# Layer 0 aggregates normalized tokens first and applies its weights behind each panel

## The chip, the core and the metric

The kernel runs on one core of one Trainium2 chip. The metric is the time of one execution on the device, in microseconds. Three runs of the kernel before took 1234.97, 1236.31 and 1237.64 us; the median is 1236.31 us.

Engines are named as the profile names them: PE is TensorE (PEld its weight load), DVE is VectorE, ACT is ScalarE, POOL is GpSimd and SP is SyncE, which issues most DMAs.

## The reference, cut to what matters

3327 tokens with 256 features pass two layers; each layer is a graph step and a mixture of experts. The change is in the graph step of layer 0, the first work of the program:

```python
# --- layer 0 ---
#   support = layernorm(x) @ W
#   out = relu(adj @ support + b)
x = x + _L0_gnn_ref(_layernorm(x, axis=-1), adj, L0_gnn_W, L0_gnn_b)
x = x + _L0_ffn_ref((_layernorm(x, axis=-1))[None], ...)[0]    # 8 experts, 2 per token, hidden 1024, ReLU
# --- layer 1: the same two kinds of step, adjacency filtered by tanh(adj * adj) and top 700 ---
```

`adj @ (layernorm(x) @ W)` equals `(adj @ layernorm(x)) @ W`, so the product with the weights can stand on either side of the aggregation. Layer 1 keeps at most 700 neighbours of a node, so the kernel counts the positive entries of each row of `adj` while it has them in memory.

## The kernel before, in words

All matrices are fp32. Tokens are padded to 3328: 26 tiles of 128 tokens, held in `x` as `[128, 26, 256]`. The transposed adjacency is cut into 13 panels of 256 nodes (`PW`); a panel holds all 3328 source tokens in two pieces of 13 tiles each (`CJ`), 1.66 MB a piece. Pieces live in a ring of six places (`RING`), so three panels are in memory at a time.

**The program is scheduled by a list scheduler at build time.** It orders the instructions of each engine by the order of the code and by its own estimate of when they are ready; every engine's queue, SP's and POOL's included, is then worked strictly in order. `tc.issue_after(ins)` and the helper `behind(list)` force what is traced inside them to come later than a given instruction on its engine's queue. DMAs of SP are issued in order, and one whose target place is not free holds all those behind it.

**Start (lines 132 to 150, 239 to 254, 1044 to 1062).** SP loads `x` in groups of tiles and the weights `proj_sb`; then the six pieces of panels 0 to 2. PE runs 32 small bf16 products on a constant (`WARM`). POOL loads biases and four small arrays of layer 1 (`f1_r_sb`, `g1_bp_sb`, `f1_b1_sb`, `g1_wg_sb`). For each group of token tiles DVE computes `statistics` (`bn_stats` and `bn_aggr` for each tile, then a chain of 12 small dependent operations on the whole group, lines 270 to 279: the inverse square root of the variance by three Newton steps). PE turns every raw tile (line 305), ACT copies the turned pair out (line 306), PE multiplies by the weights, from which the column mean is taken off once (`ps_mean`, line 1053), and ACT writes the node features `s` scaled by the inverse deviation (line 318). So `s` is `layernorm(x) @ W`, ready for all 26 tiles before the first panel.

**Panels (`aggregate`, lines 345 to 368).** For each panel and each half of 128 nodes PE sums 26 products into one PSUM tile, an adjacency block stationary and `s[:, j, :]` moving (line 359). `add_relu` on DVE adds the bias and the ReLU to `x`. Then `after0(pan)` routes the panel's tokens: a layernorm, scores against eight gates by 16 `rt_product` operations on DVE (line 379), the two best, an `Exp` on ACT (line 444), and the queueing of a list. `list_waiting` works that list a panel later: two pairs of small products on PE (lines 465 and 466), some DVE work, and four scatters of token rows on POOL into the experts' lists `xlist0` in DRAM. ACT does 16 `Sign` operations per panel with a running sum (`count`, line 1069), which read the panel's pieces in the ring: a place is free for the next load only once PE and ACT are both done with it.

**Side work on the queues.** `after0(0)` turns the two gate matrices in DRAM with element-wise DMAs on SP (line 1085), loads the first with a broadcast on POOL (`load_gate`, line 247), and `fill` writes default rows into both token lists: 32 DMAs on SP (lines 1035 and 1037) from a tile that POOL prepares. At the end of the last panels the first experts' weights are loaded into free places of the ring (`layer0.load`).

**The seam to the experts (`step`, lines 934 to 946).** A step works one block of 256 rows of one expert: `first` (products into `ps_h`, bias and ReLU on ACT), then the next block's rows are turned (line 861) and copied by DVE (line 864), then `second` (products into `ps_y`, DVE, a scatter on POOL). Two steps run after the last panel, then `list_waiting` for its tokens, then the plan for the remaining blocks.

PSUM is shared by tags: `ph` (two tiles: `ps_h`, `ptb`), `py` (four: `ps_g`, `ps_s`, `ps_y`, `ps_warm`), `pt` (two).

Of the kernel before, what the change touches and what calls it, by code (L numbers as in the profile page):

```python
# [10 lines left out]
F32 = mybir.dt.float32  # L11
BF16 = mybir.dt.bfloat16
# [63 lines left out]


BEGUN, FIRST_TILES, MORE_TILES = 12, 14, 22
WARM = 32
TIERS = 3  # L80
# [10 lines left out]
def gnn_moe_two_layers(  # L91
# [38 lines left out]
    cum = state.tile([P, NT + 1, E], BF16, name="cum")  # L130

    proj_sb = const.tile([P, DC, D], F32, name="proj_sb")
    for t, n in [(0, 2)] + [(t, 4) for t in range(2, NT, 4)]:
        nc.sync.dma_start(out=x[:, t : t + n, :], in_=x_in[:, t : t + n, :])
        if t == 0:
            nc.sync.dma_start(out=proj_sb, in_=g0_w.rearrange("(c p) n -> p c n", p=P))


# [7 lines left out]
    make_identity(nc, ident)  # L146
    mean = ring[RING - 1][:, 0:P]
    nc.gpsimd.memset(mean, 1.0 / D)
    ones = const.tile([P, 1], F32, name="ones")
# [92 lines left out]

    f1_r_sb = by_feature("f1_r_sb", f1_rT)
    gates = []

    def load_gate(g):
# [4 lines left out]

    g1_bp_sb = plain("g1_bp_sb", g1_bp)
    f1_b1_sb = plain("f1_b1_sb", f1_b1)
    g1_wg_sb = by_feature("g1_wg_sb", g1_wg)

# [52 lines left out]

    def node_features(i, lhsT, w_sb, scale=None):

        ps = psy.tile([P, D], F32, name="ps_s", tag="py")
        for c in range(DC):
            nc.tensor.matmul(
                ps, lhsT=lhsT[:, c, :], rhs=w_sb[:, c, :], start=(c == 0), stop=(c == DC - 1)
            )
        if scale is None:
            return nc.scalar.copy(s[:, i, :], ps)
        return nc.scalar.activation(s[:, i, :], ps, AF.Copy, scale=scale)

# [10 lines left out]

    def piece(pan, k):
        return ring[(pan * NCHUNK + k) % RING].rearrange("p (c w) -> p c w", w=PW)

    last_piece, output_loads = [], []

    def load_panel(pan, prepare, earlier=()):

        for k in range(NCHUNK):
            a = piece(pan, k)
            with behind(earlier):  # L340
                d = nc.sync.dma_start(out=a, in_=adjT[pan, k])
            last_piece[:] = [d]
            prepare(pan, k, a)

    def aggregate(b_sb, prepare, after, loaded=0, count=None):

        for pan in range(NPAN):
            while loaded < min(pan + RING // NCHUNK, NPAN):
                load_panel(loaded, prepare)
                loaded += 1  # L350
            chunks = [piece(pan, k) for k in range(NCHUNK)]
            if count:
                count(pan, chunks)
            ps = [psy.tile([P, D], F32, name="ps_g", tag="py") for _ in range(PW // P)]
            for k in range(NCHUNK):
                for it in range(PW // P):
                    for c in range(CJ):
                        j = k * CJ + c
                        nc.tensor.matmul(  # L359
                            ps[it],  # L360
                            lhsT=chunks[k][:, c, ts(it, P)],
                            rhs=s[:, j, :],
                            start=(j == 0),
                            stop=(j == NT - 1),
                        )
            for it in range(PW // P):
                add_relu(x[:, pan * (PW // P) + it, :], ps[it], b_sb)
            after(pan)

    def rows_of(a, t0, n):  # L370
# [382 lines left out]
    def experts(xlist, ys, group, fixed, n_hidden, func, w1T, b1, w2T, b2, copy, kept=None):  # L753
# [179 lines left out]

        def step(late, end=always, place=None):

            t = len(started)
            started.append(t)
            while len(loaded) < min(t + RING // places, end):
                load(late)
            if t not in ready:  # L940
                ready[t] = turned(loaded[t][1], groups_of(t))
            _, _, w1, bb1, _, _ = loaded[t]
            hT = first(ready.pop(t), w1, bb1, groups_of(t))
            if t + 1 < min(len(loaded), end):
                ready[t + 1] = turned(loaded[t + 1][1], groups_of(t + 1), place)
            second(t, late, hT)
# [68 lines left out]
    def fill(*lists):  # L1015


        with tc.issue_after(last_feature.ins):
            wide = blk.tile([P, H // P, SB], F32, name="wide").rearrange("p h b -> p (h b)")
# [12 lines left out]
            for xlist in lists:  # L1032
                for e in range(E):
                    first = xlist[e * NP : e * NP + SB, :].rearrange("(g p) d -> p g d", p=P)
                    nc.sync.dma_start(out=first[:, :, 0:ID], in_=zeros)
                    with nc.allow_non_contiguous_dma("two elements of a partition"):
                        nc.sync.dma_start(
                            out=first[:, :, ID : ID + 1], in_=rows_f[:, e, :].unsqueeze(2)
                        )

    deviation = {}
    for t0, n0 in [(0, 2), (2, 2), (4, 4), (8, 4), (12, 6), (18, 8)]:
        _, rs = statistics(t0, n0)
        deviation.update((t0 + g, rs[:, g : g + 1]) for g in range(n0))
        for t in range(t0, t0 + n0, 2):
            xT = turned_tiles([x[:, t + g, :] for g in range(2)])
            if t == 0:  # L1050
                ps = psy.tile([P, D], F32, name="ps_mean", tag="py")
                for c in range(DC):
                    nc.tensor.matmul(
                        ps, lhsT=mean, rhs=proj_sb[:, c, :], start=(c == 0), stop=(c == DC - 1)
                    )
                nc.vector.tensor_tensor(
                    proj_sb, proj_sb, ps.unsqueeze(1).to_broadcast([P, DC, D]), ALU.subtract
                )
            for g in range(2):
                last_feature = node_features(  # L1060
                    t + g, xT[:, :, ts(g, P)], proj_sb, deviation[t + g]
                )

    def count(pan, chunks):
        with tc.issue_after(last_feature.ins):
            for k, a in enumerate(chunks):
                for i in range(PW // GROUP):
                    sign = work.tile([P, CJ, GROUP], BF16, name="sign", bufs=1)
                    nc.scalar.activation(  # L1069
                        sign, a[:, :, ts(i, GROUP)], AF.Sign, bias=below,  # L1070
                        accum_out=positive[:, pan, i, k : k + 1],
                    )
# [6 lines left out]
    def after0(pan):  # L1079
        if pan == 0:  # L1080
            with tc.issue_after(last_piece[0].ins):
                for name, w in (("gate0", f0_wgT), ("gate1", f1_rT)):
                    g = dram.tile([E, D], F32, name=name)
                    with nc.allow_non_contiguous_dma("a few thousand elements"):
                        nc.sync.dma_start(out=g.rearrange("e d -> d e"), in_=w)
                    gates.append(g)
            load_gate(gates[0])
            fill(xlist0, xlist1)
        if FREE_PAN <= pan < NPAN - 1:
            layer0.load(None)  # L1090
        t, n = PAIRS[pan]
        list_waiting()
        xn = layernorm(t, n)
# [6 lines left out]

    aggregate(gnn_b_sb, lambda pan, k, a: None, after0, count=count)

    layer0.step(None)
    layer0.step(None)
# [418 lines left out]
```

## Time and profile before

| what | value |
|---|---|
| median of three runs | 1236.31 us (1234.97 to 1237.64) |
| the profiled execution's own time | 1235.14 us |
| its span | 1233.4 us |
| PE, PEld busy | 1198.3, 1037.4 us |
| DVE, ACT, POOL busy | 698.1, 522.6, 271.7 us |
| first product of the first panel | 41.03 us |
| first product of the first expert block | 335.41 us |
| DMA, mean over the span | 196 GB/s |

Times are counted from the start of the span. In a row of the order of time come the start, the duration of the merged group, the engine, the line, the operation, its tiles (out<-in), shape and count; in brackets stands the idle time before it and what ended that. Matmuls are pipelined and their ends are modelled, so pace is read from the distance of starts. A row of windows gives each engine's busy time in a stretch, the clock granted to PE (1.00 is full), the share of the 16 DMA engines in use and what they moved. Some matmul records can be missing.

### The profile page before, as it was taken

How to read it: one execution, taken by the hardware profiler on the slowest of the kernel's cores; microseconds unless marked ns; L12 is line 12 of the kernel's file. 1: busy time of each engine (PE TensorE's matmuls, PEld its weight loads, DVE VectorE, ACT ScalarE, POOL GpSimd, SP SyncE). 2: the span in 40 equal slices, each digit the busy share in tenths (PEclk: the TensorE clock that was granted, in tenths of full speed). 3: DMA queues.
4: the chain of work that ended last, by engine and by line, in shares of the span. 5: the costliest groups of instructions: out<-in, count | busy, mean ns of one | idle time of the engine just before them, and what ended most of it. 6: DMA issues, size and time to landing. Idle time of an engine off the chain costs nothing. (4 is left out here: it accounts for less than half of the span.)

```text
span 1233.4 us, 18208 instructions
## 1 busy us (share of the span) xinstructions
PE 1198.3 (97%) x5853; PEld 1037.4 (84%) x5853; DVE 698.1 (57%) x2812; ACT 522.6 (42%) x963; POOL 271.7 (22%) x339
## 2 busy tenths in 40 slices
PE   8999999999999999999999999999999999999973
PEld 7888888888888888888888888888888888888862
DVE  6057877677664111211121167568999999786453
ACT  4869545541022222322222225896455453043331
POOL 2003131131231111111111110002323223255531
PEclk9999999999999999999999999999999999999996
DMA  9696455454167655766657657244445442477695
GB/s 349 187 241 246 176 201 176 147 191 142 63 233 231 208 195 175 240 201 204 233 179 229 224 223 268 79 167 172 164 177 195 161 158 90 128 245 248 209 288 195
DMA packets 122537, 241.59 MB, mean 196 GB/s; under 512 B 24352, under 2 KB 92992, under 8 KB 115392
## 3 DMA queue, kind: packets, MB, share of 16 engines
q1 hardware_dynamic: 107760, 205.33, 50.1%
q0 software_dynamic: 11136, 31.60, 7.0%
q10 hardware_dynamic: 3536, 3.41, 0.8%
q8 instruction: 48, 0.79, 0.3%
q14 instruction: 57, 0.47, 0.1%
HBM read 203.98 MB, written 36.33 MB: 195 GB/s over the span
## 5 line engine op out<-in xcount | busy, mean ns | idle before, releaser
L359 PE MATMUL ps_g<-s,ring 128*128 128x256 f32 x2704 | 588.2, 380 | 0.0
L359 PEld LDWEIGHTS ps_g<-s,ring 128*128 128x128 f32 x2704 | 512.0, 190 | 68.7
L873 PE MATMUL ps_h<-xT,ring 128*128 128x256 f32 (+1 forms) x1176 | 251.1, 366 | 3.3 <-ACT xT L864 2.1
L873 PEld LDWEIGHTS ps_h<-xT,ring 128*128 128x128 f32 x1176 | 205.6, 191 | 40.6 <-ACT wide L880 5.8
L880 ACT ACTIVATE wide<-ps_h,ring 128x256 f32<-128x256 f32 (+1 forms) x240 | 110.3, 460 | 283.9 <-PE ps_h L873 283.0
L379 DVE SCALAR_TENSOR_TENSOR rt_product<-xn,gate 128x256 f32<-128x256 f32 x400 | 198.0, 495 | 12.4
L912 PE MATMUL ps_y<-ring,wide 128*128 128x256 f32 x896 | 200.3, 379 | 0.0
L483 POOL DMA_INDIRECT xlist<-xn,rt_idx x104 | 106.4, 1023 | 398.6 <-DVE ln_ve L270 281.8
L912 PEld LDWEIGHTS ps_y<-ring,wide 128*128 128x128 f32 x896 | 167.1, 190 | 21.0
L1069 ACT ACTIVATE sign<-ring,below 128x416 bf16<-128x416 f32 x208 | 133.5, 642 | 66.4 <-DMA ring<-in_adjT 60.2
L483 POOL DMA_INDIRECT ys<-narrow,index x56 | 55.1, 985 | 330.9 <-DVE narrow L920 238.1
L1220 ACT ACTIVATE ring<-ring 128x3328 f32<-128x3328 f32 x22 | 65.4, 2979 | 87.2 <-DVE ring L1219 56.6
L864 DVE COPY xT<-ptb 128x512 f32<-128x512 f32 (+1 forms) x29 | 19.0, 654 | 147.0 <-PE ptb L861 147.0
L919 DVE TENSOR_TENSOR narrow<-ps_y,ring 128x256 f32<-128x256 f32 x56 | 23.8, 424 | 133.7 <-PE ps_y L912 130.7
L323 DVE TENSOR_TENSOR gnn_t<-ps_g,gnn_b_sb 128x256 f32<-128x256 f32 x52 | 21.9, 420 | 112.1 <-PE ps_g L359 99.0
L483 POOL DMA_INDIRECT ys<-wide,index x58 | 58.2, 1004 | 60.1 <-DVE wide L920 34.5
L1221 ACT ACTIVATE ring<-ring 128x3328 f32<-128x3328 f32 x22 | 65.4, 2977 | 0.6
L444 ACT ACTIVATE rt_d<-rt_d 128x2 f32<-128x2 f32 x26 | 5.3, 202 | 117.3 <-DVE rt_d L443 117.3
L912 PE MATMUL ps_y<-s,narrow 128*128 128x256 f32 (+1 forms) x200 | 49.3, 387 | 0.1
L267 DVE BATCH_NORM_STATS2 ln_st<-x 128x6 f32<-128x256 f32 x104 | 42.9, 419 | 4.0 <-DMA x<-in_x 2.9
L861 PE MATMUL ptb<-ident,ring 128*128 128x128 f32 x228 | 36.3, 279 | 5.3 <-ACT narrow L880 5.1
L1219 DVE TENSOR_SCALAR ring<-ring 128x3328 f32<-128x3328 f32 x22 | 41.3, 1883 | 0.0
(215 smaller groups left out, 964.2 us busy)
## 6 DMA issues: line engine op xcount, KB each, us to landing
ring<-in_adjT SPq DMA_DIRECT2D x52, 1664.0 KB, 7.6
ring<-in_f_w1T SPq DMA_DIRECT2D x30, 1024.0 KB, 6.2
ring<-in_f_w2T SPq DMA_DIRECT2D x30, 1024.0 KB, 8.1
ring<-xlist SPq DMA_DIRECT2D x52, 258.0 KB, 3.1
ring<-in_f_w SPq DMA_DIRECT2D x36, 256.0 KB, 3.6
ring<-ys SPq DMA_DIRECT2D x14, 512.0 KB, 4.2
ring<-in_f_b SPq DMA_DIRECT2D x34, 128.0 KB, 7.5
xlist<-wide SPq DMA_DIRECT2D x16, 257.0 KB, 6.3
```

The costliest lines, as they stand in the source:

```text
L267: nc.vector.bn_stats(out=st, in_=x[:, t0 + g, :])
L359: nc.tensor.matmul(ps[it], lhsT=chunks[k][:, c, ts(it, P)], rhs=s[:, j, :], start=(j == 0), stop=(j == NT - 1),)
L379: nc.vector.scalar_tensor_tensor(product, xn[:, g, 0, 0:D], 1.0, gate[:, e, :], ALU.mult, ALU.mult, accum_out=sc[:, g, e : e + 1],)
L483: d = nc.gpsimd.indirect_dma_start(out=a[:, :], out_offset=bass.IndirectOffsetOnAxis(ap=index, axis=0), in_=rows_, in_offset=None,)
L861: nc.tensor.transpose(pt[:, c, ts(g, P)], xb[:, g, ts(c, P)], ident)
L873: nc.tensor.matmul(ps, lhsT=w1[:, c, ts(hc, P)], rhs=xT[:, c, :], start=(c == 0), stop=(c == DC - 1),)
L880: nc.scalar.activation(hT[:, hc, :], ps, func, bias=bb1[:, hc : hc + 1])
L912: last_product[:] = [nc.tensor.matmul(ps, lhsT=hT[:, hc, ts(g, P)], rhs=w2[:, hc, :], start=(hc == 0), stop=(hc == hc_n - 1),)]
L1069: nc.scalar.activation(sign, a[:, :, ts(i, GROUP)], AF.Sign, bias=below, accum_out=positive[:, pan, i, k : k + 1],)
L1219: nc.vector.tensor_scalar(a, a, 0.0, None, ALU.max)
L1220: nc.scalar.activation(a, a, AF.Square)
L1221: nc.scalar.activation(a, a, AF.Tanh)
```

## The change

The order of weights and aggregation is swapped for layer 0.

- `s` becomes `layernorm(x)` itself, written by DVE; the transposes, the feature products, `ps_mean` and ACT's copies before the panels go. The first four groups of tiles are put strictly one behind the other on DVE's queue; the last two are not.
- `aggregate_first` sums transposed panels: `s[:, j, c]` (128 tokens, 128 features) is stationary and 256 columns of the adjacency move; each panel has two sums, one for each half of the features. Panels 0 and 1 run together, tile by tile, through their first pieces.
- When a panel's sums are complete ACT copies them out (`g`). In the next panel, after six token tiles (`BEHIND`), PE multiplies `g` by the weights, and `add_relu` and `after0` follow (`finish`). The last panel's `finish` goes between `first` and the next block's turn in the first expert step.
- SP loads `x` in five groups, with the matching parts of the first pieces of panels 0 and 1 behind the first four. The weights and the first gate's turn stand behind panel 1, the second gate's behind panel 2.
- The counts of a panel stand behind the copies of the panel before on ACT's queue. The small loads stand behind the first layernorms in the code. `fill` runs for one list at panel 1 and for the other at panel 4, behind the latest pieces. The list of panel 0 is worked together with that of panel 1. 54 products warm PE instead of 32.

```diff
+BEHIND = 5
-WARM = 32
+WARM = 54
...
-    for t, n in [(0, 2)] + [(t, 4) for t in range(2, NT, 4)]:
+    for t, n in [(0, 2), (2, 2), (4, 4), (8, CJ - 8), (CJ, NT - CJ)]:
         nc.sync.dma_start(out=x[:, t : t + n, :], in_=x_in[:, t : t + n, :])
-        if t == 0:
-            nc.sync.dma_start(out=proj_sb, in_=g0_w.rearrange("(c p) n -> p c n", p=P))
+        if t < CJ:
+            for pan in range(2):
+                nc.sync.dma_start(
+                    out=piece(pan, 0)[:, t : t + n, :], in_=adjT[pan, 0, :, t : t + n, :]
+                )
...
+    def aggregate_first(b_sb, w, w_sb, begin, count, after):
+        sums, waiting, copied = {}, [], []
+        def start(pan):
+            sums[pan] = [psy.tile([P, PW], F32, name="ps_g", tag="py") for _ in range(DC)]
+        def add(pan, j):
+            for c in range(DC):
+                nc.tensor.matmul(
+                    sums[pan][c],
+                    lhsT=s[:, j, ts(c, P)],
+                    rhs=piece(pan, j // CJ)[:, j % CJ, :],
+                    start=(j == 0),
+                    stop=(j == NT - 1),
+                )
+        def finish():
+            pan, g = waiting.pop()
+            for it in range(PW // P):
+                ps = psh.tile([P, D], F32, name="ps_o", tag="ph")
+                for c in range(DC):
+                    nc.tensor.matmul(
+                        ps, lhsT=g[:, c, ts(it, P)], rhs=w_sb[:, c, :], start=(c == 0),
+                        stop=(c == DC - 1),
+                    )
+                add_relu(x[:, pan * (PW // P) + it, :], ps, b_sb)
+            after(pan)
+        def rest(pan, first):
+            for j in range(first, NT):
+                add(pan, j)
+                if waiting and j == first + BEHIND:
+                    finish()
+            g = work.tile([P, DC, PW], F32, name="xnT", bufs=2)
+            for c in range(DC):
+                copied.append(nc.scalar.copy(g[:, c, :], sums[pan][c]))
+            waiting.append((pan, g))
+
+        loaded = RING // NCHUNK
+        for pan in range(loaded):
+            load_panel(pan, lambda pan, k, a: None, begun=1 if pan < 2 else 0)
+            if pan == 1:
+                nc.sync.dma_start(out=w_sb, in_=w.rearrange("(c p) n -> p c n", p=P))
+                with tc.issue_after(last_piece[0].ins):
+                    turn_gate(f0_wgT)
+        with tc.issue_after(last_piece[0].ins):
+            turn_gate(f1_rT)
+        for pan in range(2):
+            start(pan)
+        for j in range(CJ):
+            for pan in range(2):
+                add(pan, j)
+        for pan in range(NPAN):
+            if pan > 1:
+                start(pan)
+            if loaded < min(pan + RING // NCHUNK, NPAN):
+                load_panel(loaded, lambda pan, k, a: None)
+                loaded += 1
+            begin(pan)
+            count(pan, copied)
+            rest(pan, CJ if pan < 2 else 0)
+        return finish
...
@@ step
             hT = first(ready.pop(t), w1, bb1, groups_of(t))
+            if between:
+                between()
...
-    deviation = {}
     for t0, n0 in [(0, 2), (2, 2), (4, 4), (8, 4), (12, 6), (18, 8)]:
-        _, rs = statistics(t0, n0)
...
-            xT = turned_tiles([x[:, t + g, :] for g in range(2)])
...
-                last_feature = node_features(
-                    t + g, xT[:, :, ts(g, P)], proj_sb, deviation[t + g]
-                )
+        with behind(last_normalized if t0 < 12 else ()):
+            layernorm(t0, n0, xn=s[:, t0 : t0 + n0, :].unsqueeze(2))
+
+    with tc.issue_after(last_normalized[0].ins):
+        g1_wg_sb = by_feature("g1_wg_sb", g1_wg)
+        f1_r_sb = by_feature("f1_r_sb", f1_rT)
+        f1_b1_sb = plain("f1_b1_sb", f1_b1)
+        g1_bp_sb = plain("g1_bp_sb", g1_bp)
...
+                with behind(copied):
                     nc.scalar.activation(
-                        sign, a[:, :, ts(i, GROUP)], AF.Sign, bias=below,
+                        sign, piece(pan, k)[:, :, ts(i, GROUP)], AF.Sign, bias=below,
...
-        list_waiting()
+        if pan != 1:
+            list_waiting()
...
+    def begin(pan):
+        if pan in (1, 4):
+            fill(xlist0 if pan == 1 else xlist1)
+
+    finish_last = aggregate_first(gnn_b_sb, g0_w, proj_sb, begin, count, after0)
+
+    layer0.step(None, between=finish_last)
     layer0.step(None)
```

## The prediction

> **What bounds the kernel now.** I read the page's busy shares first, then TensorE's order of time from 4 us to the first panel, a table of windows by panel, the rows of one layernorm on VectorE, and the seam where the panels end.
>
> ```profile
> PE 1198.3 (97%) x5853; PEld 1037.4 (84%) x5853; DVE 698.1 (57%) x2812; ACT 522.6 (42%) x963; POOL 271.7 (22%) x339
> ...
> L359 PE MATMUL ps_g<-s,ring 128*128 128x256 f32 x2704 | 588.2, 380 | 0.0
> ```
>
> TensorE is busy for 97%, and its largest group, the products with the adjacency, never waits (0.0 idle). Time is won only by taking work off TensorE or by closing its gaps. The gaps lie at the start (queue of TensorE in order of time):
>
> ```profile
> 1.07 3.60 PE L144 MATMUL ps_warm<-ones_sq 128*128 128x128 bf16 x32 [1.07 <-POOL ones_sq L140]
> ...
> 7.87 3.72 PE L313 MATMUL ps_s<-proj_sb,xnT 128*128 128x256 f32 x16
> 11.42 1.04 PE L305 MATMUL pt<-ident,x 128*128 128x128 f32 x8
> 14.76 3.72 PE L313 MATMUL ps_s<-proj_sb,xnT 128*128 128x256 f32 x16 [2.30 <-ACT xnT L306]
> 18.32 1.04 PE L305 MATMUL pt<-ident,x 128*128 128x128 f32 x8
> ...
> 41.03 1.24 PE L359 MATMUL ps_g<-s,ring 128*128 128x256 f32 x5
> ```
>
> Feature products run from 7.87 to 41.03 us, with transposes and waits between them. Windows of one panel each (after the interval: its length, then busy time and count of PE, PEld, DVE, ACT, POOL, then PEclk, DMA share, GB/s):
>
> ```profile
> 154.20:176.80 22.60, 22.60 (x109) 19.82 (x108) 16.20 (x75) 11.76 (x33) 5.09 (x6) 1.00 0.49 175
> 176.80:199.40 22.60, 22.60 (x109) 19.82 (x109) 16.21 (x75) 12.15 (x35) 5.09 (x6) 1.00 0.49 175
> ```
>
> A panel is 104 matmul instructions (26 x 2 products, each fp32 product recorded as two) in 22.62 us: 0.2175 us each. VectorE fills 16.2 of it, ScalarE about 12, the DMA half: each has room. The chain that ended last covers only the final 12 us and says nothing of layer 0.
>
> **The change part by part, in TensorE's time.**
>
> *Removed.* 52 transposes at 0.13 us (8 in 1.04), the two mean products, ScalarE's wait before each feature group, and ScalarE's evictions (26 of 0.47 and 13 of 0.59 us), which were hidden except for those waits.
>
> *Moved.* Weights go behind each panel: four products of the same shape per panel, 8 x 0.2175 = 1.74 us, 13 times = 22.6 us. The feature products took the same 104 instructions, so this neither wins nor loses. Roles change in the aggregation (token slice stationary, 256 adjacency columns moving); tile shapes and counts stay, so I keep 0.2175. Alternating between accumulators costs nothing: L873 alternates every two instructions and does 32 in 7.15 us.
>
> *New start.* The first aggregation product needs tokens 0 normalized and the first two-tile pieces. x lands at 3.79 us now; its statistics take 1.0 us; then comes the 12-step chain, whose price is read undisturbed in a later panel:
>
> ```profile
> 65.27 0.17 DVE L270 TENSOR_SCALAR ln_ve<-ln_mv 128x2 f32<-128x2 f32 x1
> ...
> 67.72 0.73 DVE L289 TENSOR_SCALAR xn<-x,ln_mv,ln_guess 128x256 f32<-128x256 f32 x2
> ```
>
> 2.45 us for the chain, 0.365 per normalized tile. So 3.79 + 1.0 + 2.45 + 0.37 + 0.1 = 7.7 us to the first product. Without starvation the gain is 41.03 - 7.7 - 22.6 = 10.7 us. The 22 further warm-up products at 0.1125 us (3.60 / 32) end at 7.15 us, inside the wait for the first token; were they slower, every microsecond past 7.7 would count in full. (Cross-check: now 104 x 0.2175 + 48 x 0.13 + 4.2 us of waits = 33.0, against 41.03 - 7.87 = 33.2.)
>
> *Starvation X.* VectorE gains 26 normalizations (9.5 us), on the path here. A tile's statistics take about 0.55 us, so a strict group of n tiles costs 0.55n + 2.45 + 0.37n. First token tile of each group: (0,2) 7.65; (2,2) 12.0; (4,4) 17.3; (8,4) 23.4. TensorE needs 8 x 0.2175 = 1.74 us per token tile while two panels run together: tile 2 is wanted at 11.2 (0.8 late), tile 4 at 15.5 (1.8 late), tile 8 at 24.3 (in time), tile 12 at 31.3. The last two groups, with no order forced on them, hold 14 tiles: 14 x 0.92 + 2.45 to 4.9 after 24.5, so they end at 40 to 42; TensorE, needing 0.87 us a tile from tile 13 on, is held 0 to 2 us once. If their statistics slip into the gaps of group (8,4)'s chain, that group is 1 to 3 us later and the last ones earlier by as much. X is 2.6 at the least, about 6 if all is serial; I take 4.0, as interleaving saved VectorE time in the trace (all 26 tiles' statistics and six chains ran from 3.8 to 23.8, where 0.55 a tile and 2.45 a chain add to 29).
>
> *Loads.* To token tile 12 are 5.1 MB (13 tiles x 393 KB); the windows show 290 GB/s at 2 to 9 us and 403 to 425 from 10 to 30, so they land by some 17 us, and each part before VectorE is done with its tokens. The second halves (1.7 MB each, behind 1.7 MB of x) land by 25 and 29; wanted at 33 and 45. The weights (256 KB) come behind those, near 30 too, and are wanted at 50. SP issues four more DMAs at about 0.6 us: 2.4 us, under the transfers. The Trainium skill (DMA: Bandwidth & Descriptors, section Bandwidth) wants 1 MiB or more per DMA for 75% of peak, against which the 256 KB pieces speak. An estimate by that page, 75% of 403, gives the 5.1 MB 16.9 us from 2 us on, still ahead of tile 12, so the sum is the same by either.
>
> *Gate turns, zeros, small loads.* The first turn held its data until 48.6 us and SP stood 23.7 us in the second. They now follow panels 1 and 2, so panel 2 may be some 9 us later (near 45, wanted at 57); panel 3's load and 16 of the 32 zero-fill DMAs stand behind it on SP, panel 4's behind those. The fills took 41 to 79 us for 32; half is 19: panel 4 issues by about 65 and is wanted past 100. GpSimd repeats one fill preparation (0.9 us) and issues four small loads later (2.7 us), ahead of the gate broadcast. Panel 0's token list waits for panel 2's turn and then goes with panel 1's: eight scatters of 1.3 us on GpSimd, which has 17 us free in each panel. All that costs nothing while panels are loaded two ahead; without that cover it is up to 9 us, once.
>
> *Copies and counts.* Two copies per panel (2 x 0.47 on ScalarE) start when the panel ends; the 16 counts (12.3 us) stand behind the previous copies and end 13 us into a 24.4 us panel. The products of the weights come 24 instructions on, 5.2 us, so 4.2 us of slack: nothing. ScalarE's Exp, ready some 16.5 us after add_relu, comes at about 23 us of the next panel, just ahead of the copies: a slip up to 4 us is free.
>
> *The seam.* The last panel's weights go between the first expert block's two halves, so VectorE's chain for it starts 8.7 us later than now.
>
> ```profile
> 344.92 0.69 DVE L864 COPY xT<-ptb 128x512 f32<-128x512 f32 x1
> 351.94 0.20 ACT L444 ACTIVATE rt_d<-rt_d 128x2 f32<-128x2 f32 x1 [8.86 <-DVE rt_d L443]
> 352.57 5.45 PE L873 MATMUL ps_h<-xT,ring 128*128 128x256 f32 x24 [0.94 <-ACT wide L880]
> ```
>
> Queued behind that chain on VectorE are the second block's xT copy and the first block's outputs; today the copy slips in after nine score products. Exp holds ScalarE's ReLUs, and so TensorE, for 0.94 us. Then Exp will stand among the second block's last ReLUs, where the next block's transposes and first products cover it: 0 to 2 us, I take 0.5, so -0.4. GpSimd's reload of the weights tile for layer 1, which waited until 41.5 us, now waits for these last products; behind it stand scatters of 1 us each, for which TensorE doesn't wait in these blocks.
>
> Sum: 10.7 - 4.0 + 0.4 = 7.1 us off. The profiled execution took 1235.1 us (span 1233.4, 1.7 around it), 1.2 under the median of 1236.3; so 1228.0 there, 1228.6 when set half-way to the median.
>
> The Trainium skill (TensorE: Matmul & The Clock Gate, Part 1) has a rule that speaks against this start: after an idle window of about 3.4 us the clock halves until 3.4 us of work have passed. The trace has one 2.30 us gap, with 16 matmuls in 3.72 us before and after it, PEclk 1.00; my gaps stay under 2. If one passed 3.4, an estimate by that page adds 1.7 us: 1230.3 instead of 1228.6. No row here shows so long a gap.
>
> **The rivals.** Measuring tells about 0.2% (2.5 us).
>
> *Starved start.* The scheduler interleaves later statistics with the first chains, as now, where tile 2's features waited until 13.39 us. For: VectorE is 97% busy from 10 to 20. Against: the forced order. X = 8 to 9, gain 2 to 3: 1233.4.
>
> *No starvation*, X near 1: gain 10 to 11, 1225.2. Against: 12 dependent steps per group.
>
> *The seam, slower.* The second block's xT copy or its first ReLUs stand behind the late chain: TensorE wants xT 16.2 us into the block, the chain ends at 8.7 + 16.5 = 25.2, so 9 to 10 us are lost, net 2.5 slower: 1238.2. It decides as soon as it takes more than 7.1. Against: the copy's row at 344.92, amid the products.
>
> *Weights wait each panel.* Copies behind a late Exp or count by more than 4.2 us: each further microsecond costs 12; one eats the gain: 1234 to 1242. For: Exp held 11.3 us behind counts near 90 us. Against: those waited for a load that now comes earlier.
>
> **How the numbers follow.** Likeliest 0.64 (own range 1226 to 1231.5), starved 0.12, no starvation 0.08, seam 0.09, each panel 0.07. Faster: 0.64 + 0.08 + half of the starved 0.06 + 0.01 = 0.79; same 0.06; slower 0.15. The range runs from X near 1 with the seam's wait gone (1224.5) to the starved end (1235).
>
> **What would show it.** Right: no L305 before the panels; first aggregation product near 7.7 us; waits of TensorE on L289 adding to 3 to 6 us before 45 us; panels 24.4 us apart, no waits on ScalarE's copy; first expert block near 327 instead of 335.4. Wrong: gaps between panels, a panel pace other than 0.2175, or a wait over 2 us within the first two expert blocks.

## The result, and the profile after

The changed kernel takes 1226.85 us (median of four runs, 1225.12 to 1228.12); the kernel before, with a fourth run beside its three, 1235.89 us (1234.97 to 1237.64). The ratio is 0.9929, 95% interval 0.9914 to 0.9943: some 9 us faster. The profiled execution of the changed kernel took 1228.12 us with a span of 1226.4 us, the slowest of its four runs; against the profiled execution before (1235.14, span 1233.4) that is 7.0 us.

The busy shares and the group of the aggregation of layer 0, from the page of the changed kernel:

```profile
PE 1189.4 (97%) x5819; PEld 1030.0 (84%) x5819; DVE 706.1 (58%) x2837; ACT 511.8 (42%) x950; POOL 270.5 (22%) x341
...
L383 PE MATMUL ps_g<-ring,s 128*128 128x256 f32 x1352 | 295.6, 380 | 5.2 <-DVE s L297 5.2
```

TensorE is still busy for 97%. The products with the adjacency, half of which stand at a line of their own now, wait for 5.2 us in total, all of it for normalized tokens from VectorE. TensorE in order of time, changed kernel, first the start and then the seam to the experts:

```profile
1.07 5.15 PE L160 MATMUL ps_warm<-ones_sq 128*128 128x128 bf16 x54 [1.07 <-POOL ones_sq L156]
7.69 3.72 PE L383 MATMUL ps_g<-ring,s 128*128 128x256 f32 x16 [1.47 <-DVE s L297]
13.41 3.72 PE L383 MATMUL ps_g<-ring,s 128*128 128x256 f32 x16 [2.00 <-DVE s L297]
18.22 14.08 PE L383 MATMUL ps_g<-ring,s 128*128 128x256 f32 x64 [1.10 <-DVE s L297]
32.90 18.40 PE L383 MATMUL ps_g<-ring,s 128*128 128x256 f32 x84 [0.59 <-DVE s L297]
51.13 1.89 PE L396 MATMUL ps_o<-proj_sb,xnT 128*128 128x256 f32 x8
...
327.20 7.09 PE L941 MATMUL ps_h<-xT,ring 128*128 128x256 f32 x32
334.12 1.89 PE L396 MATMUL ps_o<-proj_sb,xnT 128*128 128x256 f32 x8
...
343.33 7.09 PE L941 MATMUL ps_h<-xT,ring 128*128 128x256 f32 x32
...
358.22 0.70 PE L941 MATMUL ps_h<-xT,ring 128*128 128x256 f32 x2
```

The first product of the aggregation stands at 7.69 us, where the kernel before began its features. It waits three times more (2.00, 1.10 and 0.59 us) and then never again until the experts begin. The weights of a panel (L396) come without a wait, and the second expert block runs its 32 products at 343.33 without the break of 0.94 us that the kernel before had. The window of one panel (columns as in the prediction):

```profile
137.07:161.44 24.37, 24.37 (x118) 21.38 (x117) 16.01 (x74) 12.61 (x36) 4.84 (x6) 1.00 0.47 163
```

The panels follow each other at 24.36 us, 1.74 more than before: the eight instructions of the weights and nothing else.

Where the time went can be followed from mark to mark. The first expert block starts 8.2 us earlier (327.20 against 335.41). The last panel's weights, 1.74 us, stand behind that mark, and the third block starts 7.6 us earlier (358.22 against 365.82). The same 7.6 us stand at the first wait of layer 1 (732.12 against 739.72) and at 1093.95 against 1101.54. In the last 130 us both kernels wait several times for single expert blocks. In two traced executions of the changed kernel these waits differ: the second is 0.35 us ahead at 1094 us and ends 2.9 us later. So 7.6 us are followed to their place; the other 1.4 us of the 9.0 between the medians lie within this scatter.

### The profile page after: what moved, and what is told of

It is laid out like the page before. It is cut to its first block, busy times and chain, and to the rows that moved or that the text cites. A ratio compares the mean times of both kernels' runs of the same rounds, so it can differ in the third digit from the quotient of the medians.

```text
span 1226.4 us, 18144 instructions
## 1 busy us (share of the span) xinstructions
PE 1189.4 (97%) x5819; PEld 1030.0 (84%) x5819; DVE 706.1 (58%) x2837; ACT 511.8 (42%) x950; POOL 270.5 (22%) x341
## 3 DMA queue, kind: packets, MB, share of 16 engines
q10 hardware_dynamic: 3536, 3.41, 0.8%
## 5 line engine op out<-in xcount | busy, mean ns | idle before, releaser
L383 PE MATMUL ps_g<-ring,s 128*128 128x256 f32 x1352 | 295.6, 380 | 5.2 <-DVE s L297 5.2
L360 PE MATMUL ps_g<-s,ring 128*128 128x256 f32 x1352 | 294.2, 380 | 0.0
L383 PEld LDWEIGHTS ps_g<-ring,s 128*128 128x128 f32 x1352 | 255.7, 190 | 40.7 <-DVE s L297 6.5
L360 PEld LDWEIGHTS ps_g<-s,ring 128*128 128x128 f32 x1352 | 256.0, 190 | 34.4
L329 DVE TENSOR_TENSOR gnn_t<-ps_o,gnn_b_sb 128x256 f32<-128x256 f32 x26 | 11.0, 424 | 82.6 <-PE ps_o L396 82.6
```

The costliest lines, as they stand in the source:

```text
L360: nc.tensor.matmul(ps[it], lhsT=chunks[k][:, c, ts(it, P)], rhs=s[:, j, :], start=(j == 0), stop=(j == NT - 1),)
L383: nc.tensor.matmul(sums[pan][c], lhsT=s[:, j, ts(c, P)], rhs=piece(pan, j // CJ)[:, j % CJ, :], start=(j == 0), stop=(j == NT - 1),)
```

## The experiments

The theory to be tested: the gain is the features' time taken off the front of the program, because aggregation starts as soon as the first token tile is normalized and the weights run at the same cost behind the panels; what is lost of it is starvation at tiles 2, 4 and 12. The rivals: the removed work alone brings the gain; the start is held by something else (order of the loads, the small loads of GpSimd, too little warming); the order written into the queues is not needed.

**The changed kernel again.** No edit.

> The changed kernel once more, beside the others of this group. Its first four runs gave 1225.1 to 1228.1 us against 1235.0 to 1237.6 before, 9.0 us between the medians, but the two profiles differ by only 7.0 us in their spans, and the first expert block starts 8.2 us earlier (327.2 against 335.4). Theory: the gain made in layer 0 is about 8 us, and what lies beyond that is scatter: 7.5 to 9 us over more runs. Rival: the rest of the program gained too: 9 us or more, with first expert blocks again near 327.

Measured: median 1228.46 us of six (1226.34 to 1231.04), ratio 0.9931 [0.9914, 0.9948]. The start has the same three waits (1.82, 1.09 and 0.46 us), the first expert block is at 326.88. The gain repeats: 7.2 us between the medians, 8.5 by the ratio. The mark of the first expert block differs by 0.3 us between these two executions of one kernel; smaller differences of it below say nothing.

**The first half of panels 0 and 1 from the last tile to the first.** The removed and the moved work stay as they are; only the overlap of normalizing and aggregating goes.

```diff
-                    start=(j == 0),
+                    start=(j == (CJ - 1 if pan < 2 else 0)),
...
-        for j in range(CJ):
+        for j in reversed(range(CJ)):
```

> The joint first half of panels 0 and 1 takes the token tiles from 12 down to 0, so TensorE's first product waits for tile 12 (near 32.8 us) and nothing of the start lies beside the normalization; the work is the same. Theory (the gain is the overlap of the first aggregation with VectorE's start, not the work taken off TensorE): 12 tiles of 1.74 us, 20.8 us, are pushed back: 1248 to 1249, some 12 us slower than the kernel before. Rival (the gain is the transposes and mean products that went, 7 us, and the copies' waits): about 1228 to 1230, still faster than before.

Measured: 1250.84 us (four runs), ratio 1.0113 [1.009, 1.0136], first expert block at 348.37, 21.2 us later than in the changed kernel. TensorE in order of time:

```profile
31.38 28.78 PE L383 MATMUL ps_g<-ring,s 128*128 128x256 f32 x123 [25.42 <-DVE s L297]
```

What follows: without the overlap the same arithmetic is slower than the kernel before by about 1%, so the removed transposes alone do not bring the gain. Some 2 us of the 21.2 are the clock, which stood at half until 35.4 us while TensorE worked from 31.38. The overlap is a condition of the gain and not a gain beside the removed work: by the cross-check in the prediction, the 10.7 us are nearly all the transposes (6.2) and the waits (4.2) that stood between the feature products, and the overlap is what lets TensorE use that time. A kernel that overlaps and keeps the transposes was not run.

**The strict order of the first four groups lifted.**

```diff
-        with behind(last_normalized if t0 < 12 else ()):
+        with nullcontext():
```

> The strict order of the first four token groups is lifted; the scheduler then puts the statistics of tokens 2 and 3 amid the first chain, and nothing else changes. Theory: VectorE stands in that chain until those tokens land at 9.5 us, so the first product comes near 12 instead of 7.7; tile 2 follows at once, tile 4 is ready near 18 and tile 12 near 32.8 as before: the waits are only placed differently and the whole loses 0 to 1.5 us. Rival (the prediction's starved start): 4 to 5 us slower than the change.

Measured: 1229.89 us (four runs), ratio 0.994 [0.9917, 0.9963], first expert block at 327.82, 0.6 us later. TensorE and VectorE in order of time, then a window (the last three columns are the granted clock, the DMA share and GB/s):

```profile
11.18 40.74 PE L383 MATMUL ps_g<-ring,s 128*128 128x256 f32 x180 [5.42 <-DVE s L297]
```

```profile
9.57 0.43 DVE L275 BATCH_NORM_STATS2 ln_st<-x 128x6 f32<-128x256 f32 x1 [2.97 <-DMA x<-in_x]
```

```profile
10.00:12.00 2.00, 0.82 (x2) 0.73 (x3) 1.90 (x13) 0.00 (x0) 0.45 (x3) 0.77 1.03 382
```

The scheduler puts statistics of tile 2 into the first group's chain; they wait 2.97 us for their load, and the first product comes 3.5 us later. But then the tokens are ahead: 180 instructions follow without a wait, and nearly all of it is made up. They take 40.74 us where 180 x 0.2175 is 39.15, since the clock was halved from 11.08 to 14.5 us behind the gap of 5.42 us; those 1.6 us are more than the whole loss. The strict order is worth 0.6 us by the mark and about 1 us by the ratios, whose intervals overlap, not the 4 to 5 us that a starved start would have cost.

**Tokens 2 and 3 loaded ahead of the first pieces.**

```diff
     for t, n in [(0, 2), (2, 2), (4, 4), (8, CJ - 8), (CJ, NT - CJ)]:
         nc.sync.dma_start(out=x[:, t : t + n, :], in_=x_in[:, t : t + n, :])
-        if t < CJ:
-            for pan in range(2):
-                nc.sync.dma_start(...)
+        if t == 2:
+            pieces_of(0, 2)
+        if 0 < t < CJ:
+            pieces_of(t, n)
```

> Only the order of two loads: tokens 2 and 3 go ahead of the first pieces of the adjacency. In the changed kernel VectorE waited for them until 9.56 us, 1.6 us after it was free, and TensorE waited 2.00 us at tile 2. Theory: that wait is the transfer's: the tokens land by 6 to 7 us, TensorE's wait at tile 2 falls to 0.5 to 1.0. But tile 12 is ready only near 32.8, because its group waits for the last load of x (landed 26.15), so the same time is waited there: the whole kernel gains 0 to 0.6 us. Rival (every microsecond of a start wait counts): 1.2 to 1.5 us faster than the change.

Measured: 1227.25 us (six runs), ratio 0.993 [0.9912, 0.9948], first expert block at 327.66. TensorE in order of time:

```profile
9.26 8.83 PE L388 MATMUL ps_g<-ring,s 128*128 128x256 f32 x32 [2.68 <-DMA ring<-in_adjT]
```

The wait only changes its name: now the pieces land last, at 9.26 us, and the first product waits for them. Whichever order the first megabyte is sent in, its last part lands at about 9.3 to 9.6 us, so neither the token's load nor the piece's alone is the cause. Behind the longer gap TensorE ran at half clock (0.50 granted from 9.4 to 12.8 us), which costs 1.7 us there and hides whatever the tokens had won.

**The four small loads of GpSimd really behind the gate's broadcast.** In the changed kernel they were still issued between 5.3 and 8.5 us.

```diff
-    with tc.issue_after(last_normalized[0].ins):
-        g1_wg_sb = by_feature("g1_wg_sb", g1_wg)
-        ...
+            with tc.issue_after(load_gate(gates[0]).ins):
+                small_loads()
```

> Only the four small loads on GpSimd: they really stand behind the gate broadcast on its queue (in the changed kernel they were issued from 5.3 to 8.5 us all the same). Theory: they slow the early transfers: the windows moved 189 and 203 GB/s from 4 to 8 us, and without them tokens 2 and 3 land 1 to 2 us earlier and the last load of x about 1 us earlier, so tile 12 starts 0.5 to 1.2 us earlier and the kernel gains as much. Rival (the loads are too small to matter: 0.27 MB): no change of the waits.

Measured: 1227.98 us (six runs), ratio 0.9932 [0.9915, 0.9949], first expert block at 326.81. VectorE in order of time:

```profile
9.61 0.75 DVE L275 BATCH_NORM_STATS2 ln_st<-x 128x6 f32<-128x256 f32 x2 [1.11 <-DMA x<-in_x]
```

Tokens 2 and 3 land at 9.61 us as before (9.56), and the transfer rates from 2 to 8 us are the same (294, 175 and 210 GB/s against 295, 189 and 203). The first product comes 0.5 us later (8.23) and the wait for tile 2 is 0.5 us shorter (1.51); the first expert block is where the repeat has it (326.88), so nothing is gained. The small loads do not delay the start.

**Token groups of 3, 3, 4 and 3.** This gives TensorE 5.2 us of work per group; the loads are cut alike and the small loads stand late.

```diff
-    for t, n in [(0, 2), (2, 2), (4, 4), (8, CJ - 8), (CJ, NT - CJ)]:
+    for t, n in [(0, 3), (3, 3), (6, 4), (10, CJ - 10), (CJ, 5), (18, 8)]:
...
-    for t0, n0 in [(0, 2), (2, 2), (4, 4), (8, 4), (12, 6), (18, 8)]:
-        with behind(last_normalized if t0 < 12 else ()):
+    for t0, n0 in [(0, 3), (3, 3), (6, 4), (10, 3), (13, 5), (18, 8)]:
+        with behind(last_normalized if t0 < 13 else ()):
```

> Takes the starvation away: token groups of 3, 3, 4, 3, 5 and 8 tiles, the late x load cut in two (5 and 8 tiles), and the four small loads queued on GpSimd behind the gate broadcast. Theory (TensorE waits because VectorE's chain and the late load of x hold the next tile; about 4.4 us in all up to tile 12): a group of 3 costs VectorE 3 x 0.92 + 2.45 = 5.2 us and feeds TensorE for 5.2, so after the first product at 8.3 to 8.6 us the waits sum to 0.5 to 1.5 us, tile 12 starts near 30 instead of 32.9 and the kernel is 2 to 3 us faster than the change. Rival (the transfers bind the start): the waits only move to DMA and the time stays within 1 us of the change.

Measured: 1227.96 us (six runs), ratio 0.9931 [0.9914, 0.9948], first expert block at 326.14. TensorE in order of time, then windows:

```profile
9.43 40.80 PE L383 MATMUL ps_g<-ring,s 128*128 128x256 f32 x180 [2.42 <-DVE s L297]
```

```profile
10.00:12.00 2.00, 2.00 (x8) 1.58 (x7) 1.66 (x9) 0.00 (x0) 0.00 (x0) 0.63 0.96 318
12.00:14.00 2.00, 2.00 (x6) 1.62 (x5) 1.65 (x11) 0.00 (x0) 0.00 (x0) 0.52 1.04 426
```

All three later waits are gone, so starvation was the right account of them. But the 180 instructions take 40.80 us where 180 x 0.2175 is 39.15: the clock was halved from 10.5 to 13.9 us, and the 1.6 us that it cost ate most of the gain: 4.3 us of starvation gone, less 1.74 for the later first product and 1.6 for the clock, leaves 1.0, and the first expert block is 1.06 us earlier.

**The same with 96 warm-up products.** Its only further edit:

```diff
-WARM = 54
+WARM = 96
```

> The kernel with groups of three, with 96 warm-up products instead of 54. There TensorE no longer waited after its first product at 9.43 us, but the first expert block came only 1.1 us earlier (326.14): the granted clock stood at 0.50 to 0.54 from 11 to 14 us, after 2.42 us without work. Theory (the idle gap before the first product halved the clock, which took back some 1.6 us): 42 more products at about 0.05 us fill the gap, the clock stays at 1.00 and the first expert block starts near 324.6, 2.5 us before that of the changed kernel; the whole is 1.5 to 3 us faster than the change, near 1225.5. Rival (the low clock is a matter of the first microseconds of load, not of the gap): the clock falls again, first block near 326.

Measured: 1225.25 us (six runs, 1224.46 to 1228.61), ratio 0.9911 [0.9893, 0.993]. TensorE in order of time:

```profile
1.07 8.17 PE L160 MATMUL ps_warm<-ones_sq 128*128 128x128 bf16 x96 [1.07 <-POOL ones_sq L156]
9.21 10.91 PE L383 MATMUL ps_g<-ring,s 128*128 128x256 f32 x48
20.60 28.76 PE L383 MATMUL ps_g<-ring,s 128*128 128x256 f32 x132 [0.47 <-DVE s L297]
```

There is no gap ahead of the first product, the granted clock is 1.00 in every window from 4 to 40 us, one wait of 0.47 us is left, and the first expert block stands at 325.25, 1.95 us earlier than in the changed kernel and 1.6 earlier than in its repeat. This version has the lowest median and ratio of all that were run. In total time its interval still overlaps that of the changed kernel; the 1.6 to 2 us are what the traces show.

**32 warm-up products, as before the change.**

```diff
-WARM = 54
+WARM = 32
```

> The change with the 32 warm-up products of before instead of 54, so TensorE stands still from about 4.8 to 7.7 us. Theory (a gap over 2.4 us halves the clock, but a start wait is paid only once): the first 16 products take 6 to 7.5 us instead of 3.7, tile 2 comes at 14 to 15 instead of 13.4, and that is given back at tiles 4 and 12, whose tokens come at 18.2 and 32.8 either way: first expert block within 0.5 us of 327, the whole the same as the change. Rival (22 more warm-up products are worth their time): 1 to 2 us slower than the change.

Measured: 1227.23 us (six runs), ratio 0.9925 [0.9906, 0.9944], first expert block at 327.28. TensorE in order of time:

```profile
7.68 5.41 PE L383 MATMUL ps_g<-ring,s 128*128 128x256 f32 x16 [3.01 <-DVE s L297]
13.37 3.72 PE L383 MATMUL ps_g<-ring,s 128*128 128x256 f32 x16 [0.28 <-DVE s L297]
```

The first 16 products take 5.41 us instead of 3.72, at half clock from 8.5 to 11.9 us, and nothing is lost: the wait for tile 2 shrinks from 2.00 to 0.28 us. Slower products in front of a wait are free, so the longer warming earned nothing in the changed kernel itself.

The next three ran on a chip on which the kernel before took 1247.36 us (nine runs), 11 us more than elsewhere. In the first of them the waits of layer 1 at 732 and 778 us stand where the changed kernel has them, within 0.1 us, and the longer waits come behind 1090 us; so the three are read by their ratios and by their rows in layer 0.

**The weights after the first token tile of the next panel instead of after six.**

```diff
-BEHIND = 5
+BEHIND = 0
```

> The weights' products follow after the first token tile of the next panel instead of after six. Theory (each panel has slack): the trace of after has both copies of a panel's sums done about 0.35 and 0.9 us after its last product, and with one token tile (0.87 us) ahead the four products need the first copy at 0.87 and the second at 1.1 to 1.3 us, so at most 0.2 us a panel, 0 to 2.5 us in all; first product of the first expert block at 327 to 329.5 us, total 1227 to 1230. Rival (cover is needed; copies stand behind other work of ScalarE in most panels): 1 us or more a panel, first expert block beyond 338, total 1238 or more.

Measured: 1237.93 us (four runs), ratio 0.9918 [0.989, 0.9946], first expert block at 326.61. TensorE in order of time:

```profile
46.23 1.89 PE L396 MATMUL ps_o<-proj_sb,xnT 128*128 128x256 f32 x8
47.95 11.39 PE L383 MATMUL ps_g<-ring,s 128*128 128x256 f32 x52
```

No wait ahead of the weights in any panel. In the trace of the changed kernel the copies start as soon as the sums are complete, and one token tile is cover enough; the lead of six tiles is reserve only.

**The counts no longer behind the copies on ScalarE's queue.**

```diff
-                with behind(copied):
+                with nullcontext():
```

> The counts no longer stand behind the previous panel's copies on ScalarE's queue; the rest is as in after. Theory (4.2 us of cover, and pieces loaded two panels ahead): no wait of TensorE at the panels, first expert block at 326.8 to 328, total 1227 to 1229. Rival (copies stuck behind counts that wait for a load of the pieces): waits of TensorE on ScalarE's copies at the first panels, up to 5 us once or 1 us a panel, total 1232 to 1240.

Measured: 1254.31 us (five runs), ratio 1.007 [1.0042, 1.0098], first expert block at 339.75, 12.6 us later. Theory and rival were both too small. TensorE, then ScalarE, in order of time:

```profile
64.66 22.61 PE L383 MATMUL ps_g<-ring,s 128*128 128x256 f32 x104
97.12 3.78 PE L396 MATMUL ps_o<-proj_sb,xnT 128*128 128x256 f32 x8 [9.85 <-ACT xnT L410]
```

```profile
86.88 0.64 ACT L1126 ACTIVATE sign<-ring,below 128x416 bf16<-128x416 f32 x1 [9.23 <-DMA ring<-in_adjT]
...
96.72 0.62 ACT L410 COPY xnT<-ps_g 128x256 f32<-128x256 f32 x2
```

The scheduler put the copies of panel 2 behind all 16 counts of panel 3 and 13 counts of panel 4. The first of the latter waits 9.23 us for a piece that SP had sent only at 78.3 us. So the copies come at 96.72, and TensorE, done with its last tile that could run at 87.3, stands for 9.85 us; it goes on at half clock until 101.5 us (3.78 instead of 1.89 us for the weights), and one more panel waits 1.24 us. In the changed kernel the same copies stand right behind the Exp (ScalarE in order of time):

```profile
83.45 0.20 ACT L512 ACTIVATE rt_d<-rt_d 128x2 f32<-128x2 f32 x1 [10.92 <-DVE rt_d L511]
83.56 0.63 ACT L410 COPY xnT<-ps_g 128x256 f32<-128x256 f32 x2
```

So this one line of the change carries more than the whole gain: without it, in the order that the scheduler then chose, the new kernel is slower than the old one.

**The last panel's weights ahead of the first expert block.**

```diff
-    layer0.step(None, between=finish_last)
+    finish_last()
+    layer0.step(None)
```

> The last panel's weights, and with them its routing, go ahead of the first expert block instead of between its halves. Theory (the place between the halves wins what the prediction's seam row showed): TensorE waits for the last copies, 0.8 to 1.2 us, and ScalarE's Exp comes back ahead of the second block's ReLUs, 0.9 us; the first product of the third block comes 1.5 to 2 us later than after's 358.2, total about 1229 to 1230. Rival (the seam is worth nothing): third block within 0.4 us of after's, total 1227 to 1228.

Measured: 1239.97 us (five runs), ratio 0.9938 [0.9916, 0.9959], third block at 360.37, 2.15 us later than in the changed kernel. TensorE, then ScalarE, in order of time:

```profile
327.56 1.99 PE L396 MATMUL ps_o<-proj_sb,xnT 128*128 128x256 f32 x8
...
343.80 1.89 PE L941 MATMUL ps_h<-xT,ring 128*128 128x256 f32 x8
347.12 5.45 PE L941 MATMUL ps_h<-xT,ring 128*128 128x256 f32 x24 [1.43 <-ACT wide L948]
```

```profile
346.50 0.20 ACT L512 ACTIVATE rt_d<-rt_d 128x2 f32<-128x2 f32 x1 [9.37 <-DVE rt_d L511]
```

The Exp is back ahead of the second block's ReLUs and holds TensorE for 1.43 us. The wait for the copies, expected at 0.8 to 1.2 us, is about 0.2 us, since two small list products run ahead. A further 0.17 us of the 2.15 was already there at 307 us. The place between the halves is worth about 2.0 us.

## Why the prediction held, step by step

1228.6 us was predicted, 1226.85 measured. By the marks up to 1094 us the gain is 7.6 us, against 7.1 in the sum; the rest of the distance lies in the scatter behind them.

- **First product at 7.7 us:** 7.69. The chain, the normalization and the first load were read rightly from rows of the kernel before.
- **Weights moved at no cost, 1.74 us a panel:** panel distance 24.36 us against 22.62, and the pace of 0.2175 us held with the roles changed. From tile 12 to the first expert block are 1352 instructions in 294.30 us, 294.06 by the pace.
- **Starvation 4.0 us (2.6 to 6):** 3.7 us by the waits, 4.3 by the pace (32.90 - 7.69 - 96 x 0.2175). The sum was right, two of its parts were not, and that they met at 4 is in part luck. Tile 2 was put 0.8 us late by VectorE's chain and came 2.00 us late, because its load landed late; tile 12 was to wait 0 to 2 us for a VectorE busy with 14 tiles, and waited 0.59 after a late load too. VectorE in order of time, changed kernel:

```profile
3.70 0.75 DVE L275 BATCH_NORM_STATS2 ln_st<-x 128x6 f32<-128x256 f32 x2 [2.52 <-DMA x<-in_x]
...
9.56 0.76 DVE L275 BATCH_NORM_STATS2 ln_st<-x 128x6 f32<-128x256 f32 x2 [1.61 <-DMA x<-in_x]
...
26.15 0.75 DVE L275 BATCH_NORM_STATS2 ln_st<-x 128x6 f32<-128x256 f32 x2 [1.30 <-DMA x<-in_x]
...
32.44 2.02 DVE L297 TENSOR_SCALAR s<-x,ln_mv,ln_guess 128x256 f32<-128x256 f32 x6
```

- **Loads, "each part before VectorE is done with its tokens":** this is the step that failed. VectorE waited 1.61 us for tokens 2 and 3 and 1.30 us for tokens 13 to 25. The sum took 290 GB/s from 2 to 9 us; the windows of the changed kernel show 189 GB/s from 4 to 6 and 203 from 6 to 8, with the DMA share at 0.74 and 0.89. The last tokens were to land ahead of the second halves of the panels; sent at 10.24, they landed at 26.15, when the windows had moved 8.4 MB, against 6.8 MB for `x` and the two first pieces, so other loads ran beside them. Tile 4 was less late (1.10 instead of 1.8) since the wait at tile 2 had already been paid, and so the total came out.
- **Small loads 2.7 us later on GpSimd:** not so. They were issued between 5.3 and 8.5 us; an order behind an instruction of VectorE did not move GpSimd's queue. The late placing, tried above, made no difference.
- **Gate turns, zeros, second half of the loads at nothing:** held. SP stood 17.3 us over panel 2's loads and sent panel 4's from 76.1 us (65 was predicted), and TensorE waited nowhere between 60 and 320 us.
- **Copies and counts at nothing, with a rival in which the weights wait each panel:** held, and the run without the order showed that the rival is real: 12.6 us at the first expert block. Its price (1234 to 1242 us) was a little low, since 1.007 of the kernel before is 1245, and its form was wrong: one long wait behind a load, instead of a small one each panel.
- **The seam, 0.4 us won:** from the first to the third block were 30.41 us and are 31.02, of which 1.74 are new: 1.1 us won. The Exp's 0.94 us went whole, where half had been put aside for a new wait. The xT copy of the second block, on which the slower rival rested, slipped in at 337.93 us between two small operations of the chain.
- **The clock rule:** its condition was too lenient. "If one passed 3.4" does not hold in the runs, as the last section shows, and "No row here shows so long a gap" overlooked the end of the kernel before: there the clock halved at 1201.4 us in a gap of 4.11 us, and at 1177.5 behind one of only 2.05 us. The 22 further warm-up products took 0.07 us each, not 0.1125, and so ended at 6.22 instead of 7.15; the changed kernel escaped with a gap of 1.47 us.

Together: 10.7 - 4.3 + 1.1 = 7.5 us by the measured terms, against 7.6 us by the marks.

## What to carry to other kernels

When a product of three factors stands at the start of a program, take the order whose first operand is ready first and give the rest a place behind a stage that is bound by the same engine: the same products, but the engine works while the first operand is still being made. Work that releases the bounding engine must not share a strictly ordered queue behind work that waits for loads; write that order down, since here a scheduler's guess cost more than the change brought. A gap closed on the engine that bounds is only won if its clock stays up; where no later wait absorbs the loss, fill the gap ahead of the first product with idle work.

## What the runs showed of the hardware that was not expected

**The clock falls after gaps much shorter than 3 us, and by a fixed grid.** With the same start as the changed kernel, the run with the weights ahead of the first expert block had its warm-up products end at 5.83 us instead of 6.22, a gap of 1.87 us, and lost its clock (windows of that kernel, granted clock third from the end):

```profile
7.75:8.00 0.25, 0.25 (x1) 0.25 (x2) 0.21 (x1) 0.00 (x0) 0.25 (x3) 0.60 0.66 229
...
11.00:11.25 0.25, 0.25 (x2) 0.16 (x2) 0.22 (x2) 0.00 (x0) 0.00 (x0) 0.57 1.04 427
```

The fall can be placed inside a window by its mean: 0.60 over 7.75 to 8.00 puts it at 7.80, 0.57 puts the rise at 11.21. That is 3.41 us. Placed in the same way, the clock was halved from 8.49 to 11.90 (32 warm-up products), 9.38 to 12.79 (tokens 2 and 3 first), 10.5 to 13.9 (groups of three), 11.08 to 14.5 (free order), and from 8.1 to 35.4 in the reversed run: 27.3 us, eight times 3.41. The work had resumed before four of these falls, so a fall follows a window of 3.41 us that had not enough work in it, wherever the gap lies. In the window before the fall at 7.80 TensorE was busy for 1.54 of 3.41 us, 45%.

The steps hold through a whole trace: in the reversed run the falls at 8.09 and 1192.52 us lie 347 steps of 3.4133 us apart. So the windows of any trace can be laid out from one of its falls. In the changed kernel, counted back from the fall at 1193.06 us, they end at 8.63, 12.04 and 15.46 us. The gap of 1.47 us lies in one of them (57% busy), and that of 2.00 us (tile 2) is split over two (81% and 60%); the clock stayed at 1.00. So is the gap of 2.30 us in the kernel before (67% and 66%). Laid out in this way over all 13 traces, where the clock stood at 1.00, every window busy for up to 40% was followed by a halved clock, and none of 49% or more was. Between them lie three: one was followed by it (the 45% above) and two were not (42% and, in the free order from 4.25 to 7.67 us, 44%), so the limit is not placed closer than that. Whether a gap of some 2 us costs the clock thus depends on where it lies in the steps, and this differed between executions: with one and the same start, five traces had their warm-up products end between 5.83 and 6.74 us, and one of the five lost its clock.

The Trainium skill (TensorE: Matmul & The Clock Gate, Part 1) gives a free-running window of 3413 ns, and the rows agree. Its advice in the same page (Why this matters for your kernels) allows idle gaps up to about 3 us; here 1.87 us was enough, and the measurement decides.

**Loads are slow from 4 to 8 us.** In the changed kernel they moved at about 200 GB/s there, and at 412 GB/s from 14 to 16; the last part of the first megabyte landed at 9.26 us in one order and at 9.56 in the other. Why the rate is low there, with the DMA share between 0.74 and 0.89, stays open.
